# Routing two half blocks at a time, evicting the row sums ahead of the weight sums, and loading and scaling an expert's bias at other places in a GAT-then-MoE layer

## The chip, the cores and the metric

The kernel runs as one launch on one NeuronCore of a Trainium2 chip. The metric is device time in microseconds (us). Beside the timed runs there is one profiled execution, from which all the rows below come. The five engines are called as in the profile: PE (TensorE; PEld is its weight load), DVE (VectorE), ACT (ScalarE), POOL (GpSimd) and SP (SyncE, which here only issues transfers).

## What is computed

One layer of two parts on 4096 rows of 256 numbers, all in fp32. `adj` is a 4096 x 4096 table of 0 and 1.

```python
x = x + gat(layernorm(x), adj, W, a1, a2, Wr, br, gamma, beta)
x = x + moe(layernorm(x), Wg, bg, W1, b1, W2, b2)

def gat(x, adj, ...):                          # 4 heads of 64
    h = einsum('nd,hdk->hnk', x, W)
    s_col, s_row = einsum('hnk,hk->hn', h, a1), einsum('hnk,hk->hn', h, a2)
    e = leaky_relu(s_row[:, :, None] + s_col[:, None, :], 0.2)
    att = softmax(where(adj > 0, e, -9e15), -1)
    out = concat_heads(att @ h)
    y = elu(out) + x @ Wr + br
    return gamma * (y - mean(y)) / sqrt(var(y) + 1e-5) + beta

def moe(x, ...):                               # 8 experts, the best 2 of each row
    top_w, top_i = top_k(x @ Wg + bg, 2); top_w = softmax(top_w)
    return sum over the row's two experts e of
        top_w[e] * (gelu(x @ W1[e] + b1[e]) @ W2[e] + b2[e])   # hidden width 1024
```

## The kernel before, in words

**Attention.** The scores of a pair of nodes factor into a number per row (`er`) and a number per column (`eb`), so the weight of a pair is one DVE instruction: a maximum with the column's number and a product with the 0/1 mask (`weigh`, L1160, 128 columns x 1024 rows for one head). The 4096 rows are cut into NR = 4 row blocks of R = 1024, each of HB = 2 half blocks of 512; the columns are cut into NT = 32 column tiles of 128. The outer loop (L1173) goes over the row blocks `a`, the inner one (L1175) over the column tiles `j`. For each of them `load_mask` (L1051) loads a tile of `adj` through SP, ACT turns it into a mask with two activations, DVE makes four weight tiles `w` (10 buffers, shared by all), and `attend` (L741) adds them up on PE: `sum_rows` (L722) into the four PSUM banks `acc` and `sum_weights` (L731) into the bank `den`. For an even `j` the rows come first, for an odd one the weights, so that two neighbouring tiles have their like matmuls side by side. The order of these matmuls on PE is written out: `queue` (L406) chains each to the one before. Everything else is placed by the framework's scheduler, by priority and an estimate of readiness, within the order in which the program emits it[...].

**Finishing a row block.** While the next row block is attended, `finish_blocks` (L887) finishes the last: a generator that is advanced once for each column tile (L1194), and twice for every odd one in the last row block (L1196). It evicts `acc` and `den` (L894, L897; the eviction adds `hbar`, which for the first block is made from PE's `pm` of `mean_of_h` at the end of that block), turns `den` on PE (`pd`, L901), and then does for one half block after the other (`finish_block`, L910): turn and scale (L923, L925), elu (L932, L933, L935), residual with row sums (L938), layer norm (L946, L952), the write of `y` to the output, and `route_block` (L746). That one normalizes again into `xe` (L754) and calls `route_rows` (L761): turn `xe` (`ptx`, L767), gate logits (`pl`, `pg`), the two best experts by some twenty small DVE instructions (L786 to L820), the place of each row in its expert's list by matmuls with 0/1 matrices (`pk`, L829, L831, which needs DVE's `on` of L826), and eight indirect DMAs on POOL that write the rows to the lists in DRAM (L879). For the first half block a table of rows missing from the lists is made as well (L848 to L875).

**Experts.** `plan_early` (L317) cuts what is listed of the first three row blocks into 17 tiles of 256 rows of one expert; `plan_rest` cuts the remainder. A job (`fetch`, L1214) is one such tile: SP loads its rows, its expert's `w1` and `w2` (1 MB each) and the bias `b2` broadcast to all partitions (`b2b`, 128 KB), the next job's ahead of this job's work, with two buffers of each. `up` (L1297) makes 8 x 2 matmuls `ph` and eight gelus on ACT into `hT`; `turn` (L1277) transposes the next job's rows; `down` (L1315) scales `b2b` by each row's share on ACT (`b2s`, L1323), makes 2 x 8 matmuls `po`, combines them on DVE into `o` (L1337) and adds `o` to the output rows by an indirect DMA on POOL (L1340). The last of the `o` stands behind a conditional (L1407) for jobs that the input may or may not need. The two half blocks of the last row block are finished by `last_block` (L990) between the first jobs; they call `route_rows` one by one.

The lines around the transfers of a job, as they stand before the change:

```python
load_first(t, i, w1)                                             # L1226, SP
nc.sync.dma_start(w2, W2[bass.ds(e, 1)].rearrange(...))          # L1229, SP
nc.sync.dma_start(b2b, b2[bass.ds(e, 1)].to_broadcast([CH, D]))  # L1232, SP
```

Of the kernel before, what the change touches and what calls it, by code (L numbers as in the profile page):

```python
# [9 lines left out]
F32 = mybir.dt.float32  # L10
# [7 lines left out]
P = 128  # L18
# [22 lines left out]
def gat_then_moe(  # L41
# [406 lines left out]
    with ExitStack() as layer:  # L448
# [292 lines left out]
        def attend(w, j, halves):  # L741

            for add in (sum_rows, sum_weights) if j % 2 == 0 else (sum_weights, sum_rows):
                add(w, j, halves)

        def route_block(b, y, total, junk):  # L746

            off, square = spread(y, total, junk)
            yield
            r = rstd_of(square, TB, 1.0 / D)  # L750
            nc.vector.tensor_tensor(off, off, r, OP.mult)
            xe = fin.tile([P, TB, RW], F32, tag="xe", name="xe", bufs=2)
            for t in range(TB):
                nc.scalar.activation(  # L754
                    xe[:, t, :D], y[:, t, :], AF.Identity,
                    bias=off[:, t : t + 1], scale=r[:, t : t + 1],
                )
            yield
            yield from route_rows(b, xe)

        def route_rows(b, xe):  # L761

            xT = large("xT").rearrange("p t d -> p (t d)").rearrange("p (c i) -> p c i", c=DC)
            for c in range(DC):
                pt = bank([P, B], "ptx")
                for t in range(TB):
                    order_of(nc.tensor.transpose(pt[:, ts(t, P)], xe[:, t, ts(c, P)], ident))  # L767
                nc.scalar.copy(xT[:, c, :], pt)
            yield

            pl = bank([P, P], "pl")
            for c in range(DC):
                for t in range(TB):
                    order_of(nc.tensor.matmul(
                        pl[ts(t, Q), :], wg[:, c, :], xT[:, c, ts(t, P)],
                        start=(c == 0), stop=(c == DC - 1),
                    ))
            lT = small.tile([P, P], F32, tag="lT", name="lT", bufs=2)
            nc.scalar.copy(lT, pl)
            if ordered[0]:  # L780
                yield
            pg = bank([P, TB, Q], "pg")
            order_of(nc.tensor.transpose(pg.rearrange("p t q -> p (t q)"), lT, ident))
            full = [P, TB, E]
            lg = small.tile(full, F32, tag="lg", name="lg")
            nc.vector.tensor_tensor(  # L786
# [4 lines left out]

            oh = small.tile([P, 2, TB, E], F32, tag="oh", name="oh")
            m = small.tile([P, 2, TB], F32, tag="mm", name="mm")
            for k in range(2):
                nc.vector.tensor_reduce(m[:, k, :], lg, AX.X, OP.max)
                o = oh[:, k]
                nc.vector.tensor_tensor(
                    o, lg, m[:, k, :].unsqueeze(2).to_broadcast(full), OP.is_equal
                )
                nc.vector.tensor_tensor(o, o, order.unsqueeze(1).to_broadcast(full), OP.mult)  # L800
                f = small.tile([P, TB], F32, tag="first", name="first")
                nc.vector.tensor_reduce(f, o, AX.X, OP.max)
                nc.vector.tensor_tensor(
                    o, o, f.unsqueeze(2).to_broadcast(full), OP.is_equal
                )
                if k == 0:
                    nc.vector.tensor_copy(xe[:, :, FIRST], f)
                    nc.vector.scalar_tensor_tensor(
                        lg, o, -BIG, lg, op0=OP.mult, op1=OP.add
                    )  # L810
            d = small.tile([P, TB], F32, tag="d", name="d")
            nc.vector.tensor_tensor(d, m[:, 1, :], m[:, 0, :], OP.subtract)

            th = small.tile([P, TB], F32, tag="th", name="th")
            nc.scalar.activation(th, d, AF.Tanh, scale=0.5)
            p1 = small.tile([P, TB], F32, tag="p1", name="p1")
            nc.vector.tensor_scalar(p1, th, -0.5, 0.5, op0=OP.mult, op1=OP.add)
            nc.vector.tensor_copy(xe[:, :, W_1], p1)
            nc.vector.tensor_scalar(xe[:, :, W_2], th, 0.5, 0.5, op0=OP.mult, op1=OP.add)
            nc.vector.scalar_tensor_tensor(  # L820
                xe[:, :, ID], p1, 0.0, token[:, ts(b, TB)], op0=OP.mult, op1=OP.add
            )
            yield

            on = small.tile([P, TB + 1, E], BF16, tag="on", name="on")
            nc.vector.tensor_tensor(on[:, :TB], oh[:, 0], oh[:, 1], OP.add)  # L826
            nc.vector.memset(on[:, TB], 0.0)
            pk = bank([P, TB + 1, E], "pk")
            order_of(nc.tensor.matmul(pk, before, on, start=True, stop=False))  # L829
            for t in range(TB):  # L830
                order_of(nc.tensor.matmul(  # L831
                    pk[:, t + 1 :, :], all1,
                    on[:, t : t + 1, :].to_broadcast([P, TB - t, E]),
                    start=False, stop=(t == TB - 1),
                ))
            rank = small.tile(full, F32, tag="rank", name="rank")
            nc.vector.tensor_tensor(
                rank, pk[:, :TB], filled.unsqueeze(1).to_broadcast(full), OP.add
            )
            nc.vector.tensor_tensor(filled, filled, pk[:, TB], OP.add)  # L840
            nc.vector.tensor_tensor(
                oh, oh, rank.unsqueeze(1).to_broadcast([P, 2, TB, E]), OP.mult
            )
            pos = small.tile([P, 2, TB], F32, tag="pos", name="pos")
            nc.vector.tensor_reduce(pos, oh, AX.X, OP.add)
            at = small.tile([P, 2, TB], I32, tag="at", name="at")
            nc.vector.tensor_copy(at, pos)
# [28 lines left out]

            for t in range(TB):
                for k in range(2):
# [8 lines left out]
        def finish_blocks(a):  # L887
# [17 lines left out]
            nc.vector.reciprocal(z, pd[:, :, :, :HB])  # L905
            yield
            for half in range(HB):
                yield from finish_block(a * HB + half, u[:, half], z[:, :, :, half])

        def finish_block(b, u, z):  # L910

# [44 lines left out]
            nc.gpsimd.dma_start(rows_of(out, b), y)  # L956
            yield from route_block(b, y, total, m)

# [30 lines left out]

        def last_block(b, u, z, given):  # L990

# [37 lines left out]
            r, _ = root_of(mv[:, :, 1], TB)  # L1029
            xe = fin.tile([P, TB, RW], F32, tag="xe", name="xe", bufs=2)  # L1030
            for t in range(TB):
# [53 lines left out]
        with tc.If(general > 0) as chosen:  # L1085

            with tc.tile_pool(name="gen", bufs=2) as work:
# [8 lines left out]
                for b in range(NB):  # L1096
# [4 lines left out]
                    for j in range(NT):  # L1101
                        if j % 2 == 0:
                            at = load_adj(work, mine, j, 2, 2)
                        off = work.tile([P, B], F32, tag="off", name="off")
                        nc.vector.tensor_scalar(
# [13 lines left out]
                    for j in range(NT):  # L1119
                        if j % 2 == 0:  # L1120
                            at = load_adj(work, mine, j, 2, 2)
                        off = work.tile([P, B], F32, tag="off", name="off")
                        nc.vector.tensor_scalar(
# [90 lines left out]
    def fetch(t, i):  # L1214

        nch = t["parts"]
        if t is early:
            xr = early_rows[i]
        else:
            xr = work.tile([CH, t["parts"], RW], F32, tag="xr", name="xr")  # L1220
            load_rows_of(t, i, xr)
        if t is early and i == 0:
            w1 = w10
        else:
            w1 = work.tile([P, DC, F], F32, tag="w1", name="w1")
            load_first(t, i, w1)  # L1226
        e = entry(t, 0, i, E - 1)
        w2 = work.tile([P, FC, D], F32, tag="w2", name="w2")
        nc.sync.dma_start(w2, W2[bass.ds(e, 1)].rearrange("o (c p) d -> p (o c) d", p=P))  # L1229

        b2b = work.tile([CH, D], F32, tag="b2b", name="b2b")
        nc.sync.dma_start(b2b, b2[bass.ds(e, 1)].to_broadcast([CH, D]))  # L1232

        job = {"t": t, "i": i, "xr": xr, "w1": w1, "w2": w2, "nch": nch, "b2b": b2b}
# [62 lines left out]
    def up(job, xT):  # L1297
# [3 lines left out]
        for f in range(FC):  # L1301
# [3 lines left out]
            for c in range(DC):  # L1305
# [3 lines left out]
                ))  # L1309
            nc.scalar.activation(hT[:, f, :], ph, AF.Gelu, bias=job["bias"][:, f : f + 1])  # L1310
        return hT
# [3 lines left out]
    def down(job, hT):  # L1315
# [4 lines left out]
        for k in range(nch):  # L1320
            bufs, mine = (2, "_last") if job["last"] else (4, "")
            b2s.append(work.tile([CH, D], F32, tag="b2s" + mine, name="b2s", bufs=bufs))
            nc.scalar.activation(b2s[k], b2b, AF.Identity, scale=share[:, k : k + 1])  # L1323
        for k in range(nch):
# [9 lines left out]
            if k + 1 == nch:  # L1334
                yield
            o = work.tile([CH, D], F32, tag="o", name="o", bufs=2 * LAG)
            given_out.append(nc.vector.scalar_tensor_tensor(  # L1337
# [8 lines left out]
    ordered[0] = True  # L1346
    u, ud = sums_out()
    b0 = (NR - 1) * HB

# [3 lines left out]
    def between(n):  # L1353
        if n == 0:
            begun.append(turn_sums(ud))
        for half in range(HB):
            if n == 2 * half:
                begun.append(last_block(
                    b0 + half, u[:, half], begun[0][:, :, :, half], given[half],
                ))  # L1360
            if n >= 2 * half and ordered[0]:
# [85 lines left out]
```

## Time and profile before

| what | value |
|---|---|
| three timed runs | 1360.15 us median (1356.09 to 1362.56) |
| the profiled execution | 1355.94 us, of which the span of its instructions is 1354.0 us |
| busy PE, PEld | 1291.2 us (95%), 682.7 us (50%) |
| busy DVE | 873.4 us (65%), of which `w` of L1160 612.7 us |
| busy ACT, POOL | 573.0 us (42%), 226.2 us (17%) |
| granted TensorE clock | 0.991 of full speed |
| attention with finishing | to about 843 us from the span's start |
| experts | from 843 us to the end |

A row of the profile names the line, the engine, the operation and what it writes and reads (out<-in). Matmuls are pipelined and their ends are modelled, so a busy PE is not a PE at its peak; where PE waits is read from the waits and from the times between starts. "Idle before" is the time for which an engine did nothing before an instruction, with what ended it. The chain is the work that ended last, followed back from the end.

### The profile page before, as it was taken

What the parts mean: (1) busy time and instruction counts of PE and PEld (TensorE: products, weight loads), DVE (VectorE), ACT (ScalarE), POOL (GpSimd) and SP (SyncE); (2) the same over time, 40 slices, a digit from 0 to 9 for tenths busy, and PEclk for the clock granted to TensorE, in tenths of its full rate; (3) what the DMA queues carried; (4) which work ended last, traced back from release to release, by engine and by line L of the source; (5) the groups of instructions that cost most, each with busy time, mean ns of one, the idle gap of its engine ahead of it and who ended that gap; (6) DMA issues with size and microseconds to landing.
All of it is one profiled execution on the core that took longest, in us unless ns stands there. A gap on an engine that the chain in (4) does not pass through costs nothing.

```text
span 1354.0 us, 19064 instructions
## 1 busy us (share of the span) xinstructions
PE 1291.2 (95%) x7053; PEld 682.7 (50%) x7053; DVE 873.4 (65%) x1830; ACT 573.0 (42%) x1031; POOL 226.2 (17%) x190
## 2 busy tenths in 40 slices
PE   4889999999999999999999999999899999999997
PEld 3423334322222222222222222888788877888886
DVE  5899887789999989899899998665111111111110
ACT  3423333346556356654456542543233332323332
POOL 1000000000030300304000221125223112122121
PEclk9999999999999999999999999999999999999999
DMA  5625233343444534444333432977766665767662
GB/s 147 213 71 186 94 104 100 110 154 102 118 126 126 186 96 138 122 130 132 101 109 98 131 100 68 349 231 228 238 186 170 185 185 132 204 181 208 196 181 44
DMA packets 109173, 202.38 MB, mean 149 GB/s; under 512 B 8560, under 2 KB 76960, under 8 KB 109064
## 3 DMA queue, kind: packets, MB, share of 16 engines
q1 hardware_dynamic: 86320, 161.24, 37.9%
q0 software_dynamic: 19360, 32.53, 11.0%
q10 hardware_dynamic: 3384, 7.23, 1.7%
q8 instruction: 59, 0.97, 0.3%
q14 instruction: 50, 0.41, 0.1%
HBM read 171.89 MB, written 29.08 MB: 148 GB/s over the span
## 4 chain that ended last, share of the span: by engine, by line
PE 71%; DVE 18%; DMA 6%; issue 3%; ACT 1%; POOLq 0%; SPq 0%; DVEq 0%; ACTq 0%
PE acc L726 23%; PE po L1331 16%; PE ph L1306 15%; DVE w L1160 12%; PE den L735 11%; DMA out<-o,ids 3%; PE pr L604 1%; PE ph L580 1%; DMA b2b<-in_L_ffn_b 1%; PE pt L1288 1%; DMA er<-parts 1%; PE ptx L767 1%; DVE y L952 1%; DVE y L946 1%; DVE y L938 1%
## 5 line engine op out<-in xcount | busy, mean ns | idle before, releaser
L1160 DVE SCALAR_TENSOR_TENSOR w<-er,eb,am 128x1024 f32<-128x1024 f32 x496 | 612.7, 1276 | 52.9 <-PE den L735 48.7
L726 PE MATMUL acc<-w,ha 128*64 128x512 f32 x2048 | 468.5, 601 | 8.2 <-DVE w L1160 6.0
L726 PEld LDWEIGHTS acc<-w,ha 128*64 128x64 f32 x2048 | 137.6, 137 | 302.3 <-issue 278.5
L1056 ACT ACTIVATE am<-adj 128x1024 bf16<-128x1024 int32 x124 | 131.0, 1058 | 277.3 <-DVE w L1160 277.3
L735 PE MATMUL den<-w,unit 128*2 128x512 f32 x2048 | 240.3, 592 | 8.3 <-DVE w L1160 8.3
L1331 PE MATMUL po<-w,hT 128*128 128x256 f32 x1088 | 242.2, 381 | 4.7 <-ACT hT L1310 4.7
L1306 PE MATMUL ph<-xT,w 128*128 128x256 f32 (+1 forms) x1056 | 241.1, 386 | 1.6 <-DVE xT L1292 0.9
L1310 ACT ACTIVATE hT<-ph,bias 128x256 f32<-128x256 f32 (+1 forms) x264 | 123.0, 477 | 257.6 <-PE ph L1306 257.4
L1331 PEld LDWEIGHTS po<-w,hT 128*128 128x128 f32 x1088 | 205.3, 191 | 32.0 <-ACT hT L1310 5.1
L1306 PEld LDWEIGHTS ph<-xT,w 128*128 128x128 f32 x1056 | 200.1, 190 | 36.4 <-DVE xT L1292 1.3
L1340 POOL DMA_INDIRECT out<-o,ids x68 | 106.3, 1563 | 356.4 <-DVE o L1337 196.9
L1337 DVE SCALAR_TENSOR_TENSOR o<-po,share,b2s 128x256 f32<-128x256 f32 x68 | 32.8, 482 | 197.9 <-PE po L1331 192.5
L735 PEld LDWEIGHTS den<-w,unit 128*2 128x2 f32 x2048 | 44.6, 84 | 179.5 <-issue 150.1
L1057 ACT ACTIVATE am<-am 128x1024 bf16<-128x1024 bf16 x124 | 131.0, 1058 | 2.8
L879 POOL DMA_INDIRECT lists<-xe,at x64 | 85.0, 1328 | 242.6 <-issue 126.7
L1292 DVE COPY xT<-pt 128x256 f32<-128x256 f32 (+1 forms) x29 | 12.6, 433 | 163.6 <-PE pt L1288 127.3
L1323 ACT ACTIVATE b2s<-b2b,share 128x256 f32<-128x256 f32 x68 | 31.5, 501 | 49.4 <-DMA b2b<-in_L_ffn_b 30.3
L956 POOL DMA_DIRECT2D out<-y x6 | 4.8, 804 | 254.3 <-issue 178.7
L186 ACT ACTIVATE m<-y,off 128x256 f32<-128x256 f32 x48 | 23.8, 496 | 18.1 <-DVE off L183 18.1
L580 PE MATMUL ph<-wall,xT 128*128 128x264 f32 x112 | 30.6, 393 | 0.3 <-DVE sc L590 0.3
L559 PE MATMUL pt<-ident,xn 128*128 128x128 f32 x64 | 12.9, 318 | 18.0 <-ACT xn L549 11.0
L604 PE MATMUL pr<-wr,xT 128*128 128x256 f32 x112 | 29.1, 385 | 0.2 <-ACT xT L563 0.2
(310 smaller groups left out, 670.5 us busy)
## 6 DMA issues: line engine op xcount, KB each, us to landing
w<-in_L_ffn_W SPq DMA_DIRECT2D x66, 1024.0 KB, 5.6
adj<-in_adj SPq DMA_DIRECT2D x128, 512.0 KB, 3.7
er<-parts ACTq DMA_DIRECT2D x3, 2048.0 KB, 10.1
b2b<-in_L_ffn_b SPq DMA_DIRECT2D x33, 128.0 KB, 5.7
early<-lists SPq DMA_DIRECT2D x16, 260.0 KB, 7.0
residual<-rb POOLq DMA_DIRECT2D x8, 512.0 KB, 4.3
rb<-residual SPq DMA_DIRECT2D x8, 512.0 KB, 4.7
out<-y POOLq DMA_DIRECT2D x8, 512.0 KB, 3.8
```

What stands on the lines that cost most here:

```text
L580: nc.tensor.matmul(ph, xT[:, c, ts(t, P)], wall[:, c, :], start=(c == 0), stop=(c == DC - 1),)
L604: nc.tensor.matmul(pr[:, t % 2, :], xT[:, c, ts(t, P)], wr[:, c, :], start=(c == 0), stop=(c == DC - 1),)
L726: queue(nc.tensor.matmul(acc[half][h // 2][ts(h % 2, K), :], ha[:, j, ts(h, K)], w[half][h], start=(j == 0), stop=(j == NT - 1),))
L735: queue(nc.tensor.matmul(den[h * Q : h * Q + HB, :], unit[:, j, h, 1 - half : 1 - half + HB], w[half][h], start=(j == 0 and half == 0), st ...
L879: ins = nc.gpsimd.indirect_dma_start(lists, bass.IndirectOffsetOnAxis(ap=at[:, k, t : t + 1], axis=0), xe[:, t, :], None,).ins
L1056: nc.scalar.activation(am, at[:, 0], AF.Relu)
L1057: nc.scalar.activation(am, am, AF.Sign)
L1160: nc.vector.scalar_tensor_tensor(wh[:, here], er[:, h, here], eb[:, j, h : h + 1], am[:, here], op0=OP.max, op1=OP.mult,)
L1306: order_of(nc.tensor.matmul(ph, job["w1"][:, c, ts(f, P)], xT[:, c, :], start=(c == 0), stop=(c == DC - 1),))
L1310: nc.scalar.activation(hT[:, f, :], ph, AF.Gelu, bias=job["bias"][:, f : f + 1])
L1331: order_of(nc.tensor.matmul(po, hT[:, f, ts(k, CH)], w2[:, f, :], start=(f == 0), stop=(f == FC - 1)))
L1340: nc.gpsimd.indirect_dma_start(job["into"], bass.IndirectOffsetOnAxis(ap=ids[:, k : k + 1], axis=0), o, None, compute_op=OP.add,)
```

## The change

1. `route_block` becomes `list_rows`, which only normalizes a half block into its half of one `xe` of 8 row tiles (one buffer, where there were two of 4 row tiles). `finish_blocks` finishes both half blocks and then calls `route_rows` once. `route_rows` takes 4 or 8 row tiles (`n`): the transposes, gate matmuls and the indirect DMAs stay as many as before for each row, the small DVE instructions are made once, twice as wide. `last_block` still routes each half block by itself, from its half of a shared `xe`.
2. In the last column tile of each row block (`j` = 31) the rows are summed first and then the weights, as for an even tile.
3. `fetch` issues the load of `b2b` before those of `w1` and `w2`.
4. `b2s` is issued after the last gelu of its own job.
5. The very last `o` has a buffer of its own; the others have 10 in place of 12. Some small tiles (`lg`, `oh`, `on`, `rank`) have two buffers in place of three; `off` in the general branch (not taken with this input) has one.

```diff
@@ attend
-            for add in (sum_rows, sum_weights) if j % 2 == 0 else (sum_weights, sum_rows):
+            rows_first = j % 2 == 0 or j == NT - 1
+            for add in (sum_rows, sum_weights) if rows_first else (sum_weights, sum_rows):
                 add(w, j, halves)
@@ route_block, now list_rows
-        def route_block(b, y, total, junk):
+        def list_rows(xe, y, total, junk):
...
-            xe = fin.tile([P, TB, RW], F32, tag="xe", name="xe", bufs=2)
...
-            yield from route_rows(b, xe)
@@ route_rows
-            xT = large("xT").rearrange("p t d -> p (t d)").rearrange("p (c i) -> p c i", c=DC)
-            for c in range(DC):
-                pt = bank([P, B], "ptx")
-                for t in range(TB):
-                    order_of(nc.tensor.transpose(pt[:, ts(t, P)], xe[:, t, ts(c, P)], ident))
-                nc.scalar.copy(xT[:, c, :], pt)
-            yield
+            n = xe.shape[1]
+            turned_rows = []
+            for g in range(0, n, TB):
+                xT = large("xT").rearrange("p t d -> p (t d)")
+                turned_rows.append(xT.rearrange("p (c i) -> p c i", c=DC))
+                for c in range(DC):
+                    pt = bank([P, B], "ptx")
+                    for t in range(TB):
+                        order_of(nc.tensor.transpose(
+                            pt[:, ts(t, P)], xe[:, g + t, ts(c, P)], ident
+                        ))
+                    nc.scalar.copy(turned_rows[-1][:, c, :], pt)
+                yield
...
-            full = [P, TB, E]
-            lg = small.tile(full, F32, tag="lg", name="lg")
+            full = [P, n, E]
+            lg = small.tile(full, F32, tag="lg", name="lg", bufs=2)
...
-            pk = bank([P, TB + 1, E], "pk")
+            pk = bank([P, n + 1, E], "pk")
             order_of(nc.tensor.matmul(pk, before, on, start=True, stop=False))
-            for t in range(TB):
+            for t in range(n):
...
@@ finish_blocks
+            xe = rows_listed()
             for half in range(HB):
-                yield from finish_block(a * HB + half, u[:, half], z[:, :, :, half])
+                yield from finish_block(
+                    a * HB + half, u[:, half], z[:, :, :, half], xe[:, ts(half, TB)]
+                )
+            yield from route_rows(a * HB, xe)
+
+        def rows_listed():
+            return fin.tile([P, HB * TB, RW], F32, tag="xe", name="xe", bufs=1)
@@ fetch
+        e = entry(t, 0, i, E - 1)
+        b2b = work.tile([CH, D], F32, tag="b2b", name="b2b")
+        nc.sync.dma_start(b2b, b2[bass.ds(e, 1)].to_broadcast([CH, D]))
         if t is early and i == 0:
             w1 = w10
         else:
             w1 = work.tile([P, DC, F], F32, tag="w1", name="w1")
             load_first(t, i, w1)
-        e = entry(t, 0, i, E - 1)
         w2 = work.tile([P, FC, D], F32, tag="w2", name="w2")
         nc.sync.dma_start(w2, W2[bass.ds(e, 1)].rearrange("o (c p) d -> p (o c) d", p=P))
-        b2b = work.tile([CH, D], F32, tag="b2b", name="b2b")
-        nc.sync.dma_start(b2b, b2[bass.ds(e, 1)].to_broadcast([CH, D]))
@@ up
-            nc.scalar.activation(hT[:, f, :], ph, AF.Gelu, bias=job["bias"][:, f : f + 1])
+            job["gelu"] = nc.scalar.activation(
+                hT[:, f, :], ph, AF.Gelu, bias=job["bias"][:, f : f + 1]
+            ).ins
@@ down
-            nc.scalar.activation(b2s[k], b2b, AF.Identity, scale=share[:, k : k + 1])
+            with tc.issue_after(job["gelu"]):
+                nc.scalar.activation(b2s[k], b2b, AF.Identity, scale=share[:, k : k + 1])
...
-            o = work.tile([CH, D], F32, tag="o", name="o", bufs=2 * LAG)
+            if job["last"] and k + 1 == nch:
+                o = work.tile([CH, D], F32, name="o_last", bufs=1)
+            else:
+                o = work.tile([CH, D], F32, tag="o", name="o", bufs=2 * LAG - 2)
```

## The prediction

> **What bounds the kernel now.** I read the page first, then the waits engine by engine, then the chain and the timeline of the places that they point to. In the page's 40 slices PE is full nearly everywhere and DVE only in the attention part; the tensor clock is not held down.
>
> ```profile
> PE   4889999999999999999999999999899999999997
> DVE  5899887789999989899899998665111111111110
> PEclk9999999999999999999999999999999999999999
> ```
>
> In the expert part, from 843 us on, PE works off jobs of 6.91 (`ph`) + 6.91 (`po`) + 0.4 us; nothing but a PE that waits can be gained there. The waits from 843 us to the end give:
>
> ```profile
> ACT b2s L1323 <- DMA b2b<-in_L_ffn_b: 30.3, 28, 7.7
> ```
>
> ACT waits for the bias in 28 places, but PE feels it once. The scheduler has put a later job's `b2s` between the sixth and the seventh gelu, so a late bias holds the last gelus, for which `po` waits. The timeline:
>
> ```profile
> 961.34 2.76 PE L1331 MATMUL po<-w,hT 128*128 128x256 f32 x12
> ...
> 967.51 0.91 ACT L1323 ACTIVATE b2s<-b2b,share 128x256 f32<-128x256 f32 x2 [7.66 <-DMA b2b<-in_L_ffn_b]
> 968.32 0.82 ACT L1310 ACTIVATE hT<-ph,bias 128x256 f32<-128x256 f32 x2
> ...
> 968.83 1.65 PE L1331 MATMUL po<-w,hT 128*128 128x256 f32 x3 [4.73 <-ACT hT L1310]
> ```
>
> In attention PE needs 3.5 us for the rows and 1.8 for the weights of a column tile, DVE 4 x 1.20 for its `w`. DVE has some 0.4 us a tile to spare, so PE leads, except while DVE also finishes a row block. PE's waits from 60 to 840 us, in which routing's own wait is small, and the wait behind the eviction comes once:
>
> ```profile
> PE den L735 <- DVE w L1160: 7.1, 10, 1.0
> PE acc L726 <- DVE w L1160: 4.8, 4, 4.0
> PE pk L829 <- DVE on L826: 2.9, 6, 0.6
> PE acc L726 <- ACT u L894: 2.2, 1, 2.2
> ```
>
> **Part 1, routing at once.** The changed kernel, built, has 75 fewer DVE instructions in the finishing of three row blocks, 25 each. What is one worth? DVE's timeline in the first of these routings:
>
> ```profile
> 369.54 0.16 DVE L817 TENSOR_SCALAR p<-th 128x4 f32<-128x4 f32 x1
> 369.60 0.17 DVE L819 TENSOR_SCALAR xe<-th 128x4 f32<-128x4 f32 x1
> 369.68 0.18 DVE L803 TENSOR_TENSOR oh<-oh,first 128x32 f32<-128x32 f32 x1
> 369.78 0.17 DVE L818 COPY xe<-p 128x4 f32<-128x4 f32 x1
> 369.85 0.16 DVE L820 SCALAR_TENSOR_TENSOR xe<-p,token 128x4 f32<-128x4 f32 x1
> 369.92 0.18 DVE L826 TENSOR_TENSOR on<-oh 128x32 bf16<-128x32 f32 x1
> ```
>
> The column of durations says 0.17, the starts lie 0.06 to 0.10 apart: 0.38 us for five, about 0.08. The Trainium skill, "VectorE: DVE Perf Modes", section "The DRAIN you can't avoid", says that the next operation does not start before the pipe of the last is empty. By that each removed instruction frees its whole duration, 75 x 0.17 = 12.8 us; by the starts it is 75 x 0.08 = 6.0 us. The starts decide. Against it stands the width: 217 ns for the one form of 128x64 against 183 for 128x32, so 34 ns for each further 32 elements, on 18 such widenings a row block: 3 x 18 x 0.034 = 1.8. DVE gains 4.2 us.
>
> How much of it reaches PE? At least three of six waits for `on` go, 3 x 0.5 = 1.5 us. At most all 4.2 of DVE's, those 1.5, and about as much again in the turns and gate matmuls that PE meets once, 7 in all. But the second half block's elementwise work now follows sooner: its `ptr` lie 6 column tiles behind the first's, before it was 12. In the first half block DVE falls behind by two waits of 1.0 and 0.9 us; if its lead isn't back in time, the second pays some 3 us more in each row block, 9 in all. In the trace DVE idles again at 358 us, four column tiles after the last of these steps, as its buffers are full; so I expect the lead to be back, and take -4.5 (range -7 to +4.5). Nothing else should hang on the move: the sixteen list writes of a row block are 16 x (1.04 + 0.3) = 21 us of POOL, and the last row block's routing ends at its column tile 18 against 23 before, far ahead of `first_tile` at 29. The single `xe` is written again only a row block later, when its writes have landed.
>
> **Part 2, rows first.** Each change between rows and weights costs PE some 0.14 us: 16 weight matmuls take 1.83, 32 take 3.54. Seven changes are added (two at three borders, one at the last): +1.0. What it frees: at the first border PE waited 2.2 us for the eviction, but that waits for `hbar`, from PE's `pm` behind all of `j` = 31, in the old order and the new. The built order differs there otherwise: `hbar` stands one `w` earlier on DVE, and ACT evicts with no mask activation (1.06 us) in front. I take -1.5 of the 2.2 (0 to -2.2). At the second and third border PE didn't wait. At the last, `ph` waits 0.36 and 0.94 us for turned rows (from 844.06); DVE starts everything there only when PE has read the last `w`, which is the end of the weights now, so this stays. The end of `den` moves behind the rows, so `ud` comes later; its `pd` has only `pm`, 0.8 us, in front of it at the first border (about 0.2 within the above). Part 2 is -0.5.
>
> **Parts 3 and 4, the bias.** In the built order `b2s` stands behind all eight gelus of its own job. The 4.73 us wait of PE goes, and 0.26 of the same kind at 850.98 in the first job: -5.0. What is late next there? `w2`, issued just ahead of that bias at 954.19, is needed 21 us later. `b2s` is needed by `o` 3.5 us after `po` starts, and takes 0.9: covered.
>
> On SP the bias passes in front of `w1` and `w2`. Its buffer is free only when ACT has scaled the bias of two jobs before, now after that job's gelus. Behind it in SP's queue stand `w1`, `w2` and the next rows; POOL's queue is not touched. Here is the cover:
>
> ```profile
> 1295.43 0.37 SPq L445 DMA_DIRECT2D w<-in_L_ffn_W  x1
> 1295.57 6.78 PEld L1331 LDWEIGHTS po<-w,hT 128*128 128x128 f32 x32
> ```
>
> `w1` is issued when `po` starts, used at 1316.84, and lands in 5.3 us (at most 9.4 in the run). So it can be 12 us late. In a plain job the new wait lasts some 2 us (last gelu, copy, two `b2s`); at the jobs in which the last half blocks are routed one `b2s` stands behind copies or behind DVE's `d`, 4 to 5 us. Cost nothing; without cover each microsecond beyond 12 would be paid per job.
>
> **Part 5, the last `o`.** At the end DVE sat idle for the conditional's DMA waits and POOL then for DVE:
>
> ```profile
> 1347.52 0.48 DVE L1337 SCALAR_TENSOR_TENSOR o<-po,share,b2s 128x256 f32<-128x256 f32 x1 [5.38 <-DMA out<-o,ids]
> 1348.40 1.54 POOL L1340 DMA_INDIRECT out<-o,ids  x1 [4.45 <-DVE o L1337]
> ```
>
> With its own buffer DVE can combine when PE ends, at 1345.1 + 0.4. But in the built kernel POOL keeps its own waits for all landings, which last to 1347.66. So POOL issues perhaps at 1347.9: -0.5 (0 to -2.4). Ten buffers are five jobs, 71 us; a scatter lands within 9.5, and POOL's longest jam here (list writes and zeros, 934 to 959 us) is 25: no cost.
>
> **The sum.** -4.5 - 0.5 - 5.0 - 0.5 = -10.5. Against the profiled execution's own 1355.94 (span 1354.0 + 1.9 around it): 1345.4. Against the median, 1360.15: 1349.7. The runs spread over 6.5 us. The bias transfers took 4.9 to 10.7 us to land, and each one that is late by as much as the one above costs PE 5, so I think that the spread is partly such waits, and that the changed kernel comes nearer to the lower end: 1347, between the two. That is an estimate.
>
> **Rivals.**
> - *As summed* (1343 to 1352): 0.62.
> - *The second half block comes too soon*: part 1 gives nothing or costs up to 4.5; -6 to -1.5, so 1351 at the middle of the runs, up to 1358. For it: DVE is 97% busy there, with 0.4 us a tile to spare. Against it: the idle at 358 us. 0.20.
> - *The bias was worse in the timed runs*: two or three such waits in each, and all of part 1: 1339. For it: 28 waits and the spread; against it: one wait of PE in the run that is shown. 0.13.
> - *SP's queue holds the weights* (slower): `b2b` waits for ACT ahead of `w1`. It decides from 12 us of hold on. If the hold were 13 to 14 us in each of some 30 jobs, PE would lose 1 to 2 us in each, 30 to 60 us less the 10.5: 1380 and more. Against it: the last gelu ends 1 us after `po` begins. 0.05.
>
> That the change doesn't do what it says is excluded for `b2s` and the 75 instructions by the built order.
>
> The range: 1339 to 1356 leaves out the slower rival, the edge of the second and below the third. What a measurement can tell from no change is about 0.5%, 6.8 us: faster means below 1353.4. Of the first case nearly all, of the second two thirds, all of the third: 0.60 + 0.13 + 0.13 = 0.86; same 0.09; slower 0.05.
>
> **What would show it.** Right: no `po` waits for `hT` by a `b2b`; ACT's `b2s` has no DMA wait; three `pk` waits instead of six; 75 DVE instructions fewer; POOL's last issue 2.8 us behind PE's end (3.3 before). Wrong: PE's waits for `w` grow above 12 us; the border at 287 us keeps its 2.2; a `ph` waits for `w1`.

## The result and the profile after

The changed kernel takes 1340.62 us (median of 4 runs, 1339.36 to 1344.22); the kernel before, run beside it, 1359.28 (4 runs, 1356.09 to 1362.56). The ratio is 0.9867, 95% interval 0.9836 to 0.9898: 18.7 us less, where the sum of the forecast was 10.5 and the predicted time, set below that sum's, was 1347. The profiled execution of the changed kernel took 1340.80 us, with a span of 1339.2.

I cut both spans at the same events: the first `acc` of each row block, the first transposed expert rows, PE's last `po`. Row block 1 holds the first projections and moves with the initial loads; PE's wait for the eviction at the first border lies at its end, ahead of the first `acc` of row block 2, in every profile. Behind that wait PE sometimes starts row block 2 at half the granted clock. Row blocks 3 and 4 are steadier: in the four kernels in which nothing of attention was touched (the one before and three below), row block 3 took 186.34 or 186.35 us.

| kernel | row block 2 | row block 3 | row block 4 | experts | tail |
|---|---|---|---|---|---|
| before | 184.60 | 186.35 | 184.12 | 502.03 | 8.90 |
| changed | 181.12 | 181.07 | 182.19 | 497.93 | 8.82 |

So 10.7 us came from attention, row blocks 2 to 4 (forecast 5.0 for parts 1 and 2), 4.1 from the experts (forecast 5.0), nothing from the tail (0.5). These are the lines of the page that answer to those of before: the one slice of PE in the expert part that stood at 8 tenths, with the wait of 4.73 us in it, is gone.

```profile
PE   4889999999999999999999999999999999999997
DVE  5889877888999989999899996655111111111110
```

PE's waits from 60 to 840 us, read as before (total, times, longest):

```profile
PE den L735 <- DVE w L1177: 4.0, 6, 1.0
PE acc L726 <- DVE w L1177: 3.7, 3, 3.4
...
PE ptr L941 <- ACT y L943: 1.3, 3, 0.7
PE pk L840 <- DVE on L837: 1.2, 3, 0.4
...
PE acc L726 <- ACT u L905: 0.6, 1, 0.6
```

The wait of `den` for `w` fell from 7.1 to 4.0, that for `on` from 2.9 to 1.2 with three places in place of six, and the 2.2 us behind the eviction became 0.6. A wait of `ptr` for the evicted turns is new (1.3, it was 0.4). In the experts no `po` waits for a gelu any more, but another wait has come:

```profile
PE ph L1321 <- ACT hT L1325: 2.3, 2, 1.7
```

At the end DVE combines at once, and POOL sends no sooner:

```profile
1330.60 0.48 DVE L1359 SCALAR_TENSOR_TENSOR o_last<-po,share,b2s 128x256 f32<-128x256 f32 x1 [3.14 <-PEq L1431]
1333.64 1.54 POOL L1362 DMA_INDIRECT out<-o_last,ids  x1 [4.17 <-issue]
```

PE ended at 1330.34, so POOL's last issue stands 3.3 us behind it, as before.

### The profile page after: what moved, and what is told of

The parts are those of the page before. It is cut to its first block, busy times and chain, and to the rows that moved or that the text cites. A ratio compares the mean times of both kernels' runs of the same rounds, so it can differ in the third digit from the quotient of the medians.

```text
span 1339.2 us, 18923 instructions
## 1 busy us (share of the span) xinstructions
PE 1286.6 (96%) x7050; PEld 682.0 (51%) x7050; DVE 867.5 (65%) x1755; ACT 576.9 (43%) x1028; POOL 230.4 (17%) x190
## 3 DMA queue, kind: packets, MB, share of 16 engines
q0 software_dynamic: 19360, 32.53, 10.9%
## 4 chain that ended last, share of the span: by engine, by line
PE 75%; DVE 16%; DMA 5%; issue 3%; ACT 1%; POOLq 0%; SPq 0%; DVEq 0%; ACTq 0%
PE acc L726 24%; PE po L1350 16%; PE ph L1321 16%; PE den L735 12%; DVE w L1177 10%; DMA out<-o,ids 3%; PE pr L604 1%; PE ph L580 1%; PE pt L1303 1%; DMA er<-parts 1%; DVE y L964 1%; DVE y L956 1%; PE pt L559 1%; DVE y L953 1%; PE acc L633 1%
## 5 line engine op out<-in xcount | busy, mean ns | idle before, releaser
L1325 ACT ACTIVATE hT<-ph,bias 128x256 f32<-128x256 f32 (+1 forms) x264 | 126.6, 481 | 296.0 <-PE ph L1321 294.1
L890 POOL DMA_INDIRECT lists<-xe,at x64 | 89.8, 1403 | 133.6 <-DVE missed L869 39.5
L186 ACT ACTIVATE m<-y,off 128x256 f32<-128x256 f32 x48 | 23.8, 497 | 10.5 <-DVE off L183 10.5
```

Of the source, the lines that this page charges most:

```text
L890: ins = nc.gpsimd.indirect_dma_start(lists, bass.IndirectOffsetOnAxis(ap=at[:, k, t : t + 1], axis=0), xe[:, t, :], None,).ins
L1325: job["gelu"] = nc.scalar.activation(hT[:, f, :], ph, AF.Gelu, bias=job["bias"][:, f : f + 1]).ins
```

## The experiments

My theory after the result: of part 1 the place is what counts (no routing between the two half blocks' elementwise steps), not the 75 DVE instructions from which I had worked out its gain. The rival is the count. For the bias: the order on ACT against the earlier load. Twelve kernels were run, each timed against the kernel before beside it. The stages of their profiled executions:

| kernel | ratio to before (95%) | row block 2 | 3 | 4 | experts | tail |
|---|---|---|---|---|---|---|
| `route_only` | 0.9917 (0.9901 to 0.9934) | 182.43* | 180.80 | 182.13 | 502.62 | 8.82 |
| `route_moved` | 0.9903 (0.9887 to 0.9920) | 182.30* | 181.42 | 181.13 | 502.81 | 8.90 |
| `rows_only` | 0.9985 (0.9975 to 0.9994) | 184.81 | 186.61 | 184.18 | 501.53 | 9.00 |
| `bias_only` | 0.9956 (0.9940 to 0.9973) | 186.30* | 186.35 | 184.11 | 495.10 | 9.03 |
| `scale_only` | 0.9941 (0.9923 to 0.9959) | 187.54* | 186.35 | 184.11 | 495.10 | 8.93 |
| `load_only` | 0.9975 (0.9963 to 0.9988) | 184.60 | 186.34 | 184.10 | 497.94 | 8.93 |
| `before_w9` | 1.0067 (1.0045 to 1.0090) | 188.96† | 190.48† | 186.47 | 501.78 | 9.01 |
| `moved_w9` | 0.9947 (0.9926 to 0.9967) | 184.77* | 183.57 | 182.69 | 503.01 | 8.35 |
| `route_spread` | 0.9907 (0.9882 to 0.9931) | 182.66* | 180.45 | 183.32 | 502.35 | 8.60 |
| `split` | 0.9869 (0.9846 to 0.9892) | 181.97 | 181.51 | 184.10 | 495.19 | 8.79 |
| `split_tail` | 0.9881 (0.9843 to 0.9919) | 181.96 | 181.51 | 184.09 | 495.19 | 8.84 |
| `phase` | 0.9877 (0.9860 to 0.9893) | 181.88 | 181.86 | 182.21 | 495.38 | 9.73 |

\* begins at half the granted clock: the first 16 matmuls of its row sums take 8.6 to 10.1 us, where they take 7.13 in all the others. That is 1.5 us more in `route_only` and `route_moved`, 1.6 in `moved_w9`, 1.7 in `bias_only` and `route_spread`, 2.95 in `scale_only`.

† holds a stretch at half clock further on, 1.65 us each by the starts of its matmuls.

### `route_only` and `route_moved`: the place or the count

`route_only` is part 1 alone. `route_moved` makes the same move and routes each half block by itself:

```diff
-            yield from route_rows(a * HB, xe)
+            for half in range(HB):
+                yield from route_rows(a * HB + half, xe[:, ts(half, TB)])
```

> Part 1 alone: both half blocks are finished, then routed at once; columns, biases and scaling as before; the combined rows have 10 buffers in place of 12 (for space). Row blocks 2 to 4 of attention took 184.6 + 186.4 + 184.1 = 555.1 us before and 181.1 + 181.1 + 182.2 = 544.4 in the changed kernel. All theories of the gain: 545 to 548 here, 8 to 10 us less than before; the rest of the 10.7 is part 2's. If part 2 had made the gain, or needs part 1: 552 or more. The expert part stays at 502 us, the wait of po for a late bias among it; the whole about 9 us less than before, 0.993.

> As route_only, but each half block is routed by itself, one after the other, behind the second half block's elementwise steps: the move without the joining, and no DVE instruction fewer than before. My theory now (the place counts: with no routing between the two half blocks' elementwise steps DVE has its lead back when the second begins, and the turns and gate matmuls split PE's stretches later): most of route_only's gain stays, row blocks 2 to 4 sum to 546 to 550 us. The rival (the count: 75 instructions fewer are DVE's 4 to 13 us): nothing stays, 554 to 555. The prediction's own fear (the second half block too soon): 556 to 564.

Row blocks 2 to 4 sum to 545.4 and 544.9 us, before to 555.1; without the half clock at the start of row block 2, which the profile of the kernel before does not have, they are 11.2 and 11.7 us shorter than before. The timed runs say 11.3 (9.0 to 13.4) and 13.2 (10.9 to 15.3). DVE has 1755 instructions in the one, 1830 in the other, as in the kernel before, and the one with more is no slower. (`route_only` has 10 buffers of `o`, `route_moved` 12; their experts took 502.6 and 502.8 us.) The count is worth nothing that can be seen; the place is worth all of part 1.

Where PE's time went can be seen from its starts. In row blocks 2 to 4, from before to `route_moved`, the intervals within the weight sums lost 6.7 us, those ahead of a `pk` 3.0, those ahead of a `ptx` (beyond the usual 0.52) 1.4; what else changed comes to 1.0 us more, with the half clock of 1.5 in it. In the kernel before ten intervals within the weight sums are longer than 0.6 us (a usual one is 0.41), in `route_moved` three. One place, PE's timeline at the tiles 8 and 9 of row block 3, first in the kernel before, then in `route_moved`:

```profile
522.17 1.90 PE L735 MATMUL den<-w,unit 128*2 128x512 f32 x16
524.95 1.90 PE L735 MATMUL den<-w,unit 128*2 128x512 f32 x16 [0.88 <-DVE w L1160]
```

```profile
520.38 1.90 PE L735 MATMUL den<-w,unit 128*2 128x512 f32 x16
522.21 0.66 PE L942 MATMUL ptr<-ident,u 128*128 128x128 f32 x4
523.15 1.90 PE L735 MATMUL den<-w,unit 128*2 128x512 f32 x16 [0.28 <-DVE w L1178]
```

PE sums the weights of an even tile and of the next odd one back to back, and for the second it needs four further `w` in 1.8 us. In both kernels the pair takes 4.60 us from its start to the next `acc`, since DVE sets the pace. But in `route_moved` four turns of the second half block lie inside it and cost nothing; before they were paid later.

### `rows_only`

The diff is that of `attend` alone.

> Part 2 alone. As forecast: the wait behind the eviction at the first border falls from 2.2 to about 0.7 us, seven more changes between rows and weights cost 1.0; in all -0.5, row blocks 2 to 4 together 554 to 555 us. If part 2 carries more of the 10.7 us of the attention part than I gave it: 550 to 552.

It is 2.0 us faster (0.8 to 3.4). The wait behind the eviction fell from 2.2 to 0.6, row blocks 2 to 4 became 0.1 to 0.3 longer, 0.5 in all. These two make 1.1. The list of waits leaves out what can follow that wait. The two windows below begin 1.4 to 2 us behind the first `acc` of row block 2; the first is of the kernel before, the second of `route_only`, and the column PEclk, behind POOL's, is the granted clock:

```profile
core 0: us, PE busy (x) PEld busy (x) DVE busy (x) ACT busy (x) POOL busy (x), PEclk, DMA share, GB/s
290.00:292.00 2.00, 2.00 (x16) 0.41 (x16) 0.00 (x0) 0.59 (x1) 0.00 (x0) 1.00 0.10 39
```

```profile
290.00:292.00 2.00, 2.00 (x8) 0.57 (x6) 0.00 (x0) 1.23 (x2) 0.00 (x0) 0.57 0.43 166
```

Seven profiles have the wait of 2.2 us, and five of them start row block 2 at half clock, which costs 1.5 to 2.95 us; five have the wait of 0.6, and none does. So a part of the 2.0 is probably such stretches that some of the timed runs of the kernel before hold. Its own profile is one of the two without, so this is not shown.

### `bias_only`, `scale_only`, `load_only`

Parts 3 and 4 together, part 4 alone and part 3 alone, with the edits of the change's diff in `fetch`, `up` and `down`.

> Parts 3 and 4 alone: the bias loaded ahead of the weights and scaled behind the gelus. As forecast: no po wait for hT, the expert part 502.0 to 497.0 us, the whole 5 less (0.996). The rival that timed runs had two or three such waits: 8 to 15 less (0.989 to 0.994). If ACT's stalls in the gelus beside the list writes (1.7 and 2.4 us late in the changed kernel) come with the bias's new place: they are seen here too, and the expert part is 498 to 499. If they come with the joined routing or by chance: not here.

> Part 4 alone: the bias is still loaded behind the weights, but scaled behind the gelus. Both parts together took the expert part from 502.0 to 495.1 us: the wait of po (4.7) and, right behind it, about ten matmuls at half the granted clock (some 1.7). If the order on ACT is what held po: 495 to 496 here as well, while ACT still waits for DMA by the bias in some 20 places. If the late load alone made it: po's wait goes but o comes late, 497 to 502.

> Part 3 alone: the bias is loaded ahead of the weights, and its scaling stays where the scheduler puts it, between a job's gelus. If the order on ACT is needed: a part of the wait stays, 497 to 502 us. If an earlier load suffices (the transfer was late because 2 MB of weights stood in front of it): 495 to 496, and no DMA wait of ACT by the bias. If the bias holds the weights in SP's queue, ph waits for w1 and it is over 502.

Both parts: 6.0 us (3.7 to 8.1), the experts from 502.03 to 495.10, and no stall of ACT among the gelus. The scaling alone does all of it (495.10 too; 8.0 us in the timed runs, 5.6 to 10.5), and there ACT doesn't wait for the bias even once, which I had expected in some 20 places: behind the gelus it has landed. The load alone takes 4.1 of the 6.9 (3.4 in the timed runs, 1.6 to 5.0). What is left is in the first job, where `b2s` now stands in front of the gelus and its bias is late. From its timeline:

```profile
847.06 0.91 ACT L1321 ACTIVATE b2s<-b2b,share 128x256 f32<-128x256 f32 x2 [3.96 <-DMA b2b<-in_L_ffn_b]
847.98 1.28 ACT L1308 ACT_TABLE_LOAD   x1
...
849.80 1.56 PE L1304 MATMUL ph<-xT,w 128*128 128x256 f32 x6 [2.59 <-ACT hT L1308]
```

Why 6.9 where the wait was 4.73 + 0.26? The windows of the kernel before, two microseconds each, have the granted clock in the column behind POOL's:

```profile
core 0: us, PE busy (x) PEld busy (x) DVE busy (x) ACT busy (x) POOL busy (x), PEclk, DMA share, GB/s
...
968.00:970.00 2.00, 1.17 (x3) 0.99 (x4) 0.00 (x0) 1.40 (x5) 0.41 (x1) 0.68 0.24 95
970.00:972.00 2.00, 2.00 (x7) 1.55 (x6) 0.48 (x1) 0.00 (x0) 1.16 (x1) 0.50 0.16 11
972.00:974.00 2.00, 2.00 (x11) 1.77 (x9) 0.00 (x0) 0.00 (x0) 0.00 (x0) 0.97 0.40 55
```

And those of `scale_only`, at the same place:

```profile
968.00:970.00 2.00, 2.00 (x11) 1.77 (x10) 0.42 (x1) 0.00 (x0) 0.00 (x0) 1.00 0.94 354
970.00:972.00 2.00, 2.00 (x12) 1.74 (x11) 0.61 (x4) 0.00 (x0) 0.00 (x0) 1.00 0.22 88
```

Behind the 4.73 us in which PE stood, one `po` starts 0.59 and six 0.43 us after the one before, in place of 0.21: 7 matmuls per 2 us, not 11 or 12. That is 1.7 us (6 x 0.22 + 0.38) that no wait shows.

### `before_w9`, `moved_w9` and `route_spread`: is it DVE's lead?

My next theory was that DVE's lead, at most the ten buffers of `w`, pays for a half block's steps, and that the kernel before spends it twice in a row block, with DVE idle at full buffers in between. In the first two kernels `bufs=10` of `w` became `bufs=9`; the third is `route_only` with

```diff
+                if half == 0:
+                    for i in range(6):
+                        yield
```

behind `finish_block`, so that the second half block's steps come as late as they did before, with nothing between.

> The kernel before with 9 buffers for w in place of 10, so that DVE can be at most 9 weight tiles ahead of PE. My theory is that DVE's full lead is what pays for the elementwise steps of a half block and that in the kernel before it is spent twice in a row block, with DVE idle at full buffers between the two: then each of the six half blocks finished beside attention costs one w (1.2 us) more, row blocks 2 to 4 555.1 to 561 or 563 us. If the lead isn't what counts (a place on PE, or the waits for on and for xe): within 1 us.

> route_moved with 9 buffers for w. By the theory of the lead it is spent once in a row block here, as DVE doesn't reach its full lead between the two half blocks: 3 x 1.2 us more than route_moved's 544.9, so 548 to 549.5, half of what it costs the kernel before. If the two half blocks each draw on a lead of their own here too: 551 to 553. If the lead isn't what counts: within 1 us.

> route_only with six column tiles of nothing between the two half blocks: the second half block's steps come as late as in the kernel before, but no routing lies between, and the routing is still joined. It tells two readings of part 1's 10 us apart. If DVE's full buffers are what counts (it idles between the half blocks and then falls behind a second time): the waits of den for w near column tiles 17 and 19 come back, two of 1.1 to 1.3 us in a row block, row blocks 2 to 4 from 545.4 to 550 to 552 us. If the routing between the half blocks is what cost: it stays at 545 to 546. (No such wait in the last row block, where the finishing goes two steps in every second tile: then 549 to 550.)

Over row blocks 2 to 4, one buffer less costs the kernel before 10.8 us (565.9) and `route_moved` 6.2 (551.0). But `before_w9` holds two stretches at half clock, at 402.5 and 518.6 us, each behind a wait of `den` for `w` of 2.0 to 2.2 us. A window of the second, PEclk 0.50:

```profile
520.00:522.00 2.00, 2.00 (x10) 0.53 (x6) 2.00 (x5) 0.02 (x1) 0.00 (x0) 0.50 0.76 248
```

Without them, and without the half clock at the start of row block 2 in `route_moved` and `moved_w9`, it is 7.5 and 6.1. The first is what I expected (six times 1.2). The second is not the half of it that a lead spent once would cost (3 to 4.6), but nearly the same: it agrees with the rival in which the two half blocks draw on a lead each (551 to 553). The timed runs say 9.1 and 6.0 (the second from two groups of runs). The waits from 290 to 830 us, in `before_w9` (7.1 in 10 places with ten buffers, by the same window) and in `moved_w9` (3.5 in 6):

```profile
PE den L735 <- DVE w L1160: 12.2, 11, 2.2
```

```profile
PE den L735 <- DVE w L1178: 7.0, 11, 1.6
```

So the lead does limit, in the one kernel as in the other. `route_spread` too goes against the second half of the theory. There DVE is back at full buffers and idles again ahead of the second half block, in its timeline from 553 us:

```profile
566.58 7.41 DVE L1180 SCALAR_TENSOR_TENSOR w<-er,eb,am 128x1024 f32<-128x1024 f32 x6 [1.42 <-PE den L735]
```

and yet row block 3 takes 180.45 us, not the 183 that two returned waits would give, and only row block 4 loses 1.2. That the half blocks lie far apart, with idle time of DVE between, costs nearly nothing. The theory that the lead is spent twice falls.

### `split`, `split_tail` and `phase`: can more be had, and does the phase count?

`split` puts three more `yield` into each half block's steps (behind the elu, and in the middle of the layer norm's two loops). `split_tail` has also `next(giving, None)`, which emits the last combine and scatter, ahead of the conditional. `phase` shifts half blocks in the changed kernel:

```diff
+            if a == 1:
+                yield
             for half in range(HB):
                 yield from finish_block(...)
+                if half == 0:
+                    for i in range((5, 1, 0)[a]):
+                        yield
```

> The changed kernel with each half block's elementwise steps spread over three more column tiles (a step more behind the elu, and the layer norm's two steps halved). If the lead is what counts: DVE has about 0.5 us more of its own per tile, 1.5 us in a half block, so what is left of den's waits for w (about 1.2 us at tile 7 of each row block) goes in part: row blocks 2 to 4 from 544.4 to 540 to 543 us, the whole 0.1 to 0.3% below the changed kernel's 1340.6. If the waits that are left have another cause: 544 to 545. If the stalls of ACT among the gelus that the changed kernel's profile showed (2.6 us of PE) were chance, its expert part is 495 here, not 498.

> As split, and the last combine and scatter are issued before the conditional, not behind it. The row blocks as in split. The tail from PE's end was 8.9 us before and 8.8 in the changed kernel, with the last scatter issued 3.3 us behind PE's end in both, because GpSimd's queue first waits for all earlier scatters to land and then spends some 1.8 us on the conditional. If that queue alone held it: the scatter is issued some 1 us behind PE's end, and the tail is 6.5 to 7.5 us, if the conditional's waits do not follow it; if they do, they wait for the last scatter's landing and the tail is 8.5 to 10.

> The changed kernel with two shifts that tell by row block. In row block 2 the second half block's steps come five column tiles later, at an even tile (18) where they were at an odd one (13). In row block 3 the first half block's come one tile later (7, odd, where it was 6) and the second's two (15, odd). Row block 4 is left alone. Reading A, the phase: PE sums the weights of an even and of the next odd tile back to back, so that it asks for eight w within 3.7 us, and for no new one in the 7 us of rows that follow; a half block's heavy first steps (5.6 us of DVE in two tiles) at an even tile end just ahead of that, at an odd tile just behind it. Then row block 2 goes from 181.1 to 182.8 to 183.8 us, with two waits of den for w of about 1.1 near tiles 19 and 21, and row block 3 from 181.1 to 180.2 to 180.7, its 1.2 us wait at tile 7 gone but for some 0.5 in the rows. Reading B, only that routing no longer lies between the half blocks: both 181.0 to 181.5, and the wait at tile 7 goes along with the shift. Row block 4 by both: 182.2.

`split` made the row blocks 0.9, 0.4 and 1.9 us longer, against the expectation: thinner steps met the weight sums of more tiles. In row blocks 2 and 3 `den` waits four times for `w`, 0.4 to 0.5 us each, in place of 1.0 and 0.3; in row block 4 a `ptr`, a `den` and a `pk` wait 1.1 to 1.2 us each. `split_tail` moved the last scatter from 3.3 to 2.1 us behind PE's end, but the conditional's waits for landings then came behind it, and the tail stayed at 8.84.

`phase` agrees with neither reading in full. The wait did come at the place that the phase reading names: with the second half block at the even tile 18, PE's timeline in row block 2 has

```profile
392.83 1.90 PE L735 MATMUL den<-w,unit 128*2 128x512 f32 x16 [1.02 <-DVE w L1182]
...
403.50 0.65 PE L771 MATMUL ptx<-ident,xe 128*128 128x128 f32 x4
404.44 1.90 PE L735 MATMUL den<-w,unit 128*2 128x512 f32 x16 [0.29 <-DVE w L1182]
```

and a second one two tiles later is filled by `ptx`. But the row block is 0.8 us longer, not 1.7 to 2.7. In row block 3 the wait of 1.0 at tile 7 is gone, and the block is 0.8 longer all the same: waits of 0.3 in the rows and 0.4 in the weights stand in its place, and `ptx` now waits 1.1 us for `xe`. So the phase sets where PE waits, but shifts of this kind give nothing. None of the three is measurably faster than the changed kernel (0.987 to 0.988 of before, as it).

## Why the prediction was right or wrong

The time was in the range, but 1.6 us above its lower end, and the direction was right. Three terms were too small, that of part 1 by the most. The lower end had been set for the rival of two or three late biases in each run, and no profile shows that; without it the range would have ended at 1343. So that 1340.6 lies inside is in part luck. Of the five signs of being right four came (no `po` waits for a late bias, no DMA wait of `b2s`, three waits for `on`, 1755 DVE instructions in place of 1830); POOL's last issue did not move.

**Part 1** is the step that failed. It said: DVE's 75 instructions at 0.08 us less the width, 4.2 us net, and "at most all 4.2 of DVE's, those 1.5, and about as much again", 7 in all. The runs give 11.3. The duration of a small instruction did not matter at all: `route_moved` saves none of these instructions and has the whole gain. (I had also set 0.08, by the starts, against 0.17 as the rule of the Trainium skill, "VectorE: DVE Perf Modes", section "The DRAIN you can't avoid". That section says as well that a next operation that is not held starts earlier; the starts 0.06 to 0.10 us apart agree with that.) What I should have costed is the waits in which PE meets the finishing: those for `w` within the weight sums (6.7 us went), for `on` (3.0) and for `xe` (1.4). I had these in view as 7.1, 2.9 and a small rest, and took 1.5 of the second only. The bound of 7 was no bound, because it counted DVE's work and not PE's waits.

**The rival that the second half block comes too soon** was wrong in its direction. Coming sooner, its turns fell into a pair of weight sums in which PE would have waited. The lead wasn't back by then either (DVE did not idle between the half blocks in `route_moved`), so my reason against the rival was wrong too.

**Part 2**: -0.5 was said, -2.0 measured (-3.4 to -0.8). The step at the border was right: 2.2 fell to 0.6, where I took 1.5 off. The mis-sized term is that of the seven switches: 1.0 was forecast, row blocks 2 to 4 of `rows_only` show 0.21, 0.26 and 0.06. The half clock that can follow a wait of 2.2 us was not counted at all.

**Parts 3 and 4**: the mechanism was right, and alone they gave 6.0 (profile 6.9), not 5.0. The step that was short is "the 4.73 us wait of PE goes": behind the wait PE also ran at half the granted clock, 1.7 us more, and with them the term would have been 6.7. From the page I had read that the tensor clock is not held down; but a slice of the page is 34 us long, and 3.4 us at half clock leave its digit at 9. By the traces, half clock was granted behind each of the 21 waits of PE of 3.1 us or more that the 14 profiles hold from 70 us on, and behind eight of the seventeen between 1.3 and 2.6 us. The Trainium skill says a part of it, in "TensorE: Matmul & The Clock Gate", section "Part 1: The HAM clock gate (the "warmup" mystery)": after an idle window of about 3.4 us the array runs at half rate until it has been busy for about as long. The length agrees, 3.4 or 6.8 us in the traces; half of the page's 3.4 us gives an estimate of 1.7. But waits well under 3.4 us brought it here too, so that by the measurement 3.4 us of idling is no safe limit. In the changed kernel itself the experts fell by 4.1 only, since ACT held PE for some 2.6 us at 934 to 938 us.

I also wrote that the spread is partly such waits. That stays open. Of the 28 runs of the kernel before beside the second group, the five with a granted clock of 0.992 or more took 1351.3 to 1355.9 us, the median of those at 0.989 or less is about 1359. So the slower runs hold more half clock. But `load_only`, whose profile has no wait of `po` for a gelu, divides in the same way (medians 1351.2 and 1355.4 at these clocks), so other waits, such as that behind the eviction, take part. The rival of two or three waits in each is not needed: of the seven profiles in which the bias stood at its old place six show one wait of `po` for a gelu (3.6 to 4.8 us), and the seventh, `route_spread`, one of 3.2 us of `ph` for turned rows at the same stretch.

**The slower rival**: SP's queue is held as described. `w1` is issued 2.2 us behind the start of `po`, where it was 0.25 us ahead of it:

```profile
1280.95 7.07 PE L1350 MATMUL po<-w,hT 128*128 128x256 f32 x32
1282.28 0.34 SPq L1241 DMA_DIRECT2D b2b<-in_L_ffn_b  x1
1283.18 0.37 SPq L445 DMA_DIRECT2D w<-in_L_ffn_W  x1
```

That is the "some 2 us" of the working, the cover was 12, and no `ph` waits for `w1`.

**Part 5** gave nothing. "POOL issues perhaps at 1347.9" left out that POOL's waits for landings and its conditional's instructions stand in its queue whether or not `o` is ready.

**The sum**: the parts measured alone give 11.3 + 2.0 + 6.0 = 19.3, all together 18.7. Within their intervals they add up; no part is seen to hide behind another.

**What stays open.** The 11 to 13 us of part 1 are shown to come from the place of the routing, and not from its count or from the distance of the half blocks. How they divide between turns that fall into a wait, the phase, and the waits for `on` and `xe` is only read from the traces; the shifts that should have told it apart made both row blocks 0.8 us longer. The stall of ACT is open as well. In the changed kernel two gelus start 1.7 and 2.4 us after both their `ph` and the gelu before them had ended; the second is shown:

```profile
937.04 1.20 ACT L1325 ACTIVATE hT<-ph,bias 128x256 f32<-128x256 f32 x3 [2.38 <-PE ph L1321]
...
937.57 1.13 PE L1321 MATMUL ph<-xT,w 128*128 128x256 f32 x4 [1.72 <-ACT hT L1325]
```

The same is seen, 1.0 to 2.4 us long and at nearly no cost for PE, in `split`, `split_tail` and `phase`, always beside the last list writes, and in none of the kernels with a part of the change only. No experiment was made on it.

## What to carry to other kernels

Cost a move on a helping engine by the waits of the bounding engine that it can remove, one by one from their starts, and not by the helper's instruction count: 75 fewer instructions were worth nothing, their new place 11 us. A wait of the matrix engine has to be charged with the half-speed stretch that can follow it and that appears in no list of waits: here 1.5 to 3 us where it was measured, behind every wait of 3.1 us or more and behind half of those between 1.3 and 2.6. It also makes equal stages of two profiles differ, so it is to be taken out before they are compared. An operation that waits for a late transfer belongs behind the work of its in-order queue that others wait for; here that alone did what the earlier load did only in part.

## What the runs showed that I had not expected

- Half clock after an idle PE: 0.50 granted for 3.4 us around the end of 4.73 us of standing (1.7 us of PE), and the same 0.43 us matmuls behind 3.6 us. Of seven equal waits of 2.2 us behind the eviction five brought it, of two of 1.35 us one; 2.6 us in `load_only` did not.
- The waits as listed understate a pause within the weight sums: the list gives 1.0 us where the starts lie 1.61 apart in place of 0.41, as the end of a matmul in the profile is modelled.
- Stages without a change of clock repeat far better than whole runs: row block 3 took 186.34 or 186.35 us in four executions, so that a stage can tell half a microsecond where the whole time, with runs up to 6 us apart, cannot.
- One of ten buffers of `w` is worth 9.1 us to the kernel before (ratio 1.0067, 1.0045 to 1.0090), a part of it half clock behind the longer waits.
